# Local attention layers: keys transposed by VectorE in 32x32 blocks and DMAs instead of by TensorE, with another order of the query and key columns

## The chip, the cores and the metric

The kernel runs on one core of a Trainium2 chip. The metric is the device time of one execution in microseconds (us). The engines of the core work side by side, each through its own list of instructions in order: TensorE (PE; its weight loads are shown as PEld), VectorE (DVE), ScalarE (ACT), GpSimd (POOL) and SyncE (SP), which here issues nearly all DMAs. Sixteen DMA engines move what is issued.

## The reference, cut to what matters

The input x is 8 batches of 128 tokens of width 128. Four blocks of attention and feed-forward follow one another (L0 to L3). The change concerns the feed-forward parts of L2 and L3, which are themselves stacks of local attention layers: L2 has 6 layers with 16 heads of 64 and a window of 32, L3 has 2 layers with 8 heads and a window of 64. One layer of a stack:

```python
qkv = shift_tokens(x) @ Wqkv;  q, k, v = split(qkv)          # heads of 64
q = l2norm(q) * qs;  k = l2norm(k) * ksc
q = q * cos * scale + rotate_half(q) * sin * scale           # k: with 1 / scale
x = x + local_attention(q, k, v) @ Wo                        # softmax(8 q.k), a band of tokens
h = layernorm(shift_tokens(x)) @ W1 + b1
x = x + (a * gelu(gate)) @ W2 + b2                           # a, gate = halves of h
```

Scores sum over the 64 features of a head, so they do not depend on the order of the features, as long as queries and keys have the same order.

## The kernel before, in words

All of L2's and L3's work is one plan (`later_layers`, `plan_later`). Each step is added with `plan.add`: the engines that may do it with an assumed duration in ns (the account), the function that emits it, what it reads and writes, and for DMAs a `tail`, the time from the issue's end to landing. `Plan.arranged` then simulates the engines with this account and lets each engine take, of the steps that are ready, the one that was added first (its rank). The result is a fixed order of instructions on each engine. An instruction waits on semaphores for what it needs, and what stands behind it on its engine waits with it. SP's queue of DMA issues is such a list too.

A layer is worked batch by batch, in two parts. `Local.first` does `shifted` and `queries_keys`; `Local.rest` does `attention`. `some(n)` in `plan_later` adds the `rest` of a batch and before it the `first` of batches further on: two ahead in L2, one ahead in L3. After every two batches `gated` does the feed-forward part for the pair, and the next layer's batches become available. Weights of a layer are loaded by `weights`, alternating between two buffers. Where L2 ends, the steps of L3's cross attention (`l3x`) are woven in between the last batches of L2 and the first of L3 with `along`.

`queries_keys` handles tiles of 128 tokens x 512 columns (8 heads): in L2 two tiles of queries and two of keys per batch, in L3 one of each. Per tile: the projection on PE into PSUM (L1902), the squares on ScalarE (L1923), two products with the rotary tables on VectorE (L1924 with the cosines; L1926 with the sines, reading each head's halves swapped), the sum of squares per head on VectorE (L1928), and the sum of the two products on POOL (L1929). `inv_root` makes the inverse norms, and POOL multiplies each tile by them (L1942). Then the tile has to be transposed, features on the partitions:

- Queries go through `Blocks.turned`: VectorE transposes 32x32 blocks within the tile (L1795), SP issues four DMAs that put them, in runs of 128 floats (512 B), into a buffer in DRAM (L1799), and one DMA that reads the buffer back in rows of 2 KB (L1804). There are 8 such buffers, used in turn.
- Keys go through `Work.turn`: four TensorE transposes into a PSUM bank (L784), then a copy to SBUF by ScalarE (L771) or VectorE (L773), whichever the plan has free.

`weighed` computes the scores (band at L2010, products at L2016) and the exponentials (L2023); sums and outputs follow in `by_quarters` (L2077, L2083) or `by_halves` (L2056, L2062), the inverse (L2031 to L2040), the division (L2045), the output projection (L1991) and the update of y (L1995). In L2, `gated` moves the shifted rows by two DMAs (L2107), normalises, transposes through `Blocks.turned` as well (the tail of which is the ScalarE step at L2122), and runs the products L2132, L2146 and L2156.

Of the kernel before, what the change touches and what calls it, by code (L numbers as in the profile page):

```python
# [18 lines left out]
AF = mybir.ActivationFunctionType  # L19
ALU = mybir.AluOpType  # L20
AX = mybir.AxisListType
# [3 lines left out]
P = 128  # L25
# [59 lines left out]
def by_quarters(o):  # L85


    n = o.shape[1]
    o = o.reshape(2, 4, 2, 2, 32, n)
    return o.transpose(0, 2, 4, 3, 1, 5).reshape(P, 8 * n)  # L90


# [43 lines left out]
def laid_out(i):  # L136
# [60 lines left out]
    def local(m, qkv, wo, a, b):  # L197
# [15 lines left out]
        "experts": np.ascontiguousarray(experts), "expert_b2": i["L1_ffn_b2"],  # L213
        "l2a": l2a, "l2b": l2b, "l2o": l2o, "l3a": l3a, "l3b": l3b,
    }
# [508 lines left out]
class Work:  # L724
# [75 lines left out]
    def scaled(self, outs, ins, reads, writes, under, n=4, on_dve=False):  # L800
# [15 lines left out]

        plan.add({"POOL": (500 if on_dve else 930) + 150 * n}, root, [mv], [va] if on_dve else [va, nb])
        for k in range(n):
# [958 lines left out]
class Blocks:  # L1777
# [6 lines left out]

    def turned(self, t, n=4):

        w = self.w
        nc, plan = w.c.nc, w.plan
        room, val = self.rooms[self.turn][:, 0 : n * P], self.vals[self.turn]
        self.turn = (self.turn + 1) % len(self.rooms)  # L1790
        u, qT = w.tile([P, n * P]), w.tile([P, n * P])

        def within(e):
            flat = t().rearrange("p h d -> p (h d)")
            nc.vector.transpose(u().rearrange("p (c k j) -> p k c j", c=4, j=32), flat.rearrange("p (k c j) -> p k c j", c=4, j=32))  # L1795

        def out(e):
            for r in range(4):
                nc.sync.dma_start(room.rearrange("(c i) (r e) -> i c r e", c=4, r=4)[:, :, r, :],  # L1799
                                  u()[32 * r : 32 * r + 32].rearrange("p (c e) -> p c e", c=4))  # L1800

        plan.add({"DVE": 145 + 137 * n}, within, [t], [u])
        plan.add({"SP": 4 * 400}, out, [u], [val], tail=2100)
        plan.add({"SP": 400}, lambda e: nc.sync.dma_start(qT(), room), [val], [qT], tail=2300)  # L1804
        at = lambda k, lo, q, end, m=64: qT().rearrange("p (r k j) -> p k r j", r=4, j=32)[lo : lo + m, k, q // 32 : end // 32, :]
        return qT, at


BUFS_C = {"w": 2, "wr": 2, "tiny": 24, "few": 12, "row": 20, "big": 48}


class Local:
# [44 lines left out]
    def weights(self, l, after=(), begun=lambda load: None):  # L1857
# [14 lines left out]
        def emit(e):  # L1872
            for k, sname in enumerate(("_q_scale", "_k_scale")):
                s = c.get("row", self.name + sname, 64 * l, 64)
                nc.gpsimd.tensor_tensor(rot()[:, 2 * k, :], xpos[:, 2 * k, :], s, ALU.mult)
                for t in range(2):
                    lo, hi = 32 * t, 32 * (1 - t)
                    nc.gpsimd.tensor_tensor(rot()[:, 2 * k + 1, lo : lo + 32],
                                            xpos[:, 2 * k + 1, lo : lo + 32], s[:, hi : hi + 32], ALU.mult)

# [18 lines left out]
    def projected(self, layer, hs, j, o, opens):  # L1899
        nc = self.c.nc  # L1900
        ps, wqkv = self.bank([P, 512]), layer.wqkv
        self.plan.add({"PE": 860}, lambda e: nc.tensor.matmul(  # L1902
            ps(), lhsT=hs()[:, j, :], rhs=wqkv()[:, o : o + 512], start=True, stop=True), [hs, wqkv], [ps], "full", opens)
        return ps

    def queries_keys(self, layer, hs, j):
# [6 lines left out]
        for kind in range(2):  # L1913
            for g in range(ng):
                sq, t1, t2 = self.tile([P, 8, 64]), self.tile([P, 8, 64]), self.tile([P, 8, 64])
                ps = self.projected(layer, hs, j, kind * inner + g * 512, [t1])
                lo = 8 * (kind * ng + g)

                def emits(ps=ps, sq=sq, t1=t1, t2=t2, lo=lo, kind=kind):
                    heads = lambda: ps().rearrange("p (h d) -> p h d", d=64)  # L1920
                    halves = lambda v: v.rearrange("p h (t d) -> p h t d", t=2)
                    sin = lambda: spread(rot()[:, 2 * kind + 1, :].rearrange("p (t d) -> p t d", t=2), 8, 1)
                    yield lambda e: nc.scalar.activation(sq(), heads(), AF.Square)  # L1923
                    yield lambda e: nc.vector.tensor_tensor(t1(), heads(), spread(rot()[:, 2 * kind, :], 8, 1),  # L1924
                                                            ALU.mult)
                    yield lambda e: nc.vector.tensor_tensor(halves(t2()), halves(heads())[:, :, ::-1, :], sin(),  # L1926
                                                            ALU.mult)
                    yield lambda e: nc.vector.tensor_reduce(ss()[:, lo : lo + 8], sq(), AX.X, ALU.add)  # L1928
                    yield lambda e: nc.gpsimd.tensor_tensor(t1(), t1(), t2(), ALU.add)  # L1929

# [9 lines left out]
        for i in range(2 * ng):  # L1940
            t, t1 = self.tile([P, 8, 64]), ts[i]
            plan.add({"POOL": 1062}, lambda e, t=t, t1=t1, i=i: nc.gpsimd.tensor_tensor(  # L1942
                t(), t1(), spread(r()[:, 8 * i : 8 * i + 8], 64, 2), ALU.mult), [t1, r], [t])
            if i < ng:
                out.append(self.blocks.turned(t))
                continue
            tp = self.turn(lambda k, t=t: t().rearrange("p h d -> p (h d)")[:, k * P : (k + 1) * P], [t])
            kT = self.tile([P, 4, P])
            self.copy(kT, tp, [tp], [kT], 591, 682)
            out.append(kT)  # L1950
        return out[:ng], out[ng:]

    def inv_root(self, ss, n):

        nc, plan = self.c.nc, self.plan
        xh, r, t = (self.tile([P, n]) for _ in range(3))
        plan.add({"POOL": 240}, lambda e: nc.gpsimd.tensor_scalar(xh(), ss(), 1e-24, -0.5, ALU.max, ALU.mult), [ss], [xh])
        plan.add({"ACT": 215}, lambda e: nc.scalar.activation(t(), xh(), AF.Ln, scale=-2.0), [xh], [t], LOGS)
        plan.add({"ACT": 215}, lambda e: nc.scalar.activation(r(), t(), AF.Exp, scale=-0.5), [t], [r], LOGS)

# [18 lines left out]
    def attention(self, layer, b, hs, j, qTs, kTs):  # L1979
# [7 lines left out]
        for g, oT in enumerate(oTs):  # L1987
# [5 lines left out]

            plan.add({"PE": 890}, project, [oT, wr], [out], "full")
        plan.add({"DVE": 282}, lambda e: nc.vector.tensor_tensor(y(), y(), out(), ALU.add), [out, y], [y])  # L1995
# [31 lines left out]
    def inverse(self, sm):  # L2027

        nc, plan = self.c.nc, self.plan
        t, r = self.tile([P, 4, P]), self.tile([P, 4, P])  # L2030
        plan.add({"ACT": 597}, lambda e: nc.scalar.activation(t(), sm(), AF.Ln), [sm], [t], LOGS)  # L2031

# [4 lines left out]

        plan.add({"ACT": 632}, exp, [t], [r], LOGS)
        plan.add({"DVE": 688}, lambda e: nc.vector.tensor_tensor(sm(), sm(), r(), ALU.mult), [sm, r], [sm])
# [52 lines left out]
    def gated(self, l, b0, n, last=False):  # L2092
# [10 lines left out]
        if self.by_dma:  # L2103
# [4 lines left out]

            plan.add({"SP": 2 * 400}, move, ys, [moved], tail=2200)
            plan.add({"POOL": 150}, lambda e: nc.gpsimd.memset(sh()[0:1, :, 64:P], 0.0), [], [edge])  # L2110
# [8 lines left out]
        if self.by_dma:  # L2119
            hT, of_h = self.blocks.turned(sn, n)  # L2120
            hf = lambda: of_h(slice(0, n), 0, 0, P, P)
            plan.add({"ACT": 190 + 103 * n}, lambda e: nc.scalar.activation(hT(), hT(), AF.Identity, bias=offset, scale=gain), [hT], [hT])  # L2122
        else:
# [20 lines left out]
        for k, (lo, m) in enumerate(HCH):  # L2144
            pa, gl = self.bank([P, n * P]), gls[k]
            plan.add({"PE": 215 * n}, lambda e, pa=pa, lo=lo, m=m: nc.tensor.matmul(  # L2146
                pa()[:m], lhsT=w1()[:, lo : lo + m], rhs=hf(), start=True, stop=True), [hT, wr], [pa], "full")
            plan.add({"DVE": 145 + 150 * n}, lambda e, k=k, m=m, pa=pa, gl=gl: nc.vector.scalar_tensor_tensor(
                gl()[:m], pa()[:m], bias(k)[:m], gl()[:m], ALU.add, ALU.mult), [pa, gl], [gl])
# [62 lines left out]
def plan_later(w, route, l2x, l2, l3x, l3, stored):  # L2212
# [7 lines left out]
    def some(n):  # L2220

        for i in range(n):
            while at["first"] < min(at["rest"] + 1 + (2 if at["rest"] < 48 else 1), len(order)) and order[at["first"]] in given:
                loc, l, b = order[at["first"]]
                loc.first(l, b)
                at["first"] += 1
# [57 lines left out]
    pairs(l2, 5, 0, 4)  # L2284
    l2.end(0, 4)
    steps = l3x(0)
    along(steps, 0, 1)
    gated(l2, 5, 4, 2)
    along(steps, 1, 1)
# [4 lines left out]
    l2.end(4, 4)  # L2294
    l3.layers[1] = l3.weights(1)
    steps = l3x(1)
    for b in (0, 2):
        along(steps, 1, 1)
        gated(l3, 0, b, 2)
    for _ in steps:  # L2300
        pass
    begin(l3, 4, 4)
    pairs(l3, 0, 4, 4)
    for b, n in ((0, 1), (1, 1), (2, 1), (3, 1), (4, 2), (6, 1), (7, 1)):
# [25 lines left out]
def later_layers_any(c, a, wl, dram, route, wide, narrow, out):  # L2330
# [9 lines left out]
    with c.banks("psa_l2", mm=2, tp=2, sc=2, av=2):  # L2340
        local_layers_any(c, "L2_ffn", 6, 8, 32, a["l2a"], a["l2b"], room)
    with work(c, "l3x", BUFS_C, True) as w:
# [4 lines left out]
    with c.banks("psa_l3", mm=2, tp=2, sc=2, av=2):  # L2347
        local_layers_any(c, "L3_ffn", 2, 4, 64, a["l3a"], a["l3b"], room)
    store(c, out, 0, B)
# [43 lines left out]
```

## Time and profile before

| what | value |
|---|---|
| median of the runs | 1463.06 us (1461.44 to 1463.34, 3 runs) |
| the profiled execution, its own time | 1489.26 us |
| its span, first to last instruction | 1487.5 us |
| granted TensorE clock, mean | 0.964 |
| HBM traffic over the span | 95 GB/s |
| DMA packets | 148946, of which 34654 under 512 B |
| mean duration of a 128x512 VectorE product (L1924, L1926) | 675 ns |
| VectorE transpose of 128x512 (L1795) | 702 ns |
| POOL sum (L1929) and product (L1942) | 1276 and 1044 ns |

The profile is one execution. Its rows give, for a group of instructions: line, engine and operation, what is written <- what is read, shapes, count | busy us, mean ns of one | idle time of the engine just before them and what ended it. A row of a window gives its bounds and length, then each engine's busy time and count, the granted clock, the DMA engines' mean busy share and GB/s. A row of waits gives the total, the number and the longest, in us. A row of the chain of waits gives start, length and what the end of the program waited for at that moment.

### The profile page before, as it was taken

To read this page: it belongs to the slowest core of one execution; us is meant where nothing else is said; L and a number is where in the kernel's file an instruction comes from. 1 tells how busy PE (TensorE), PEld (TensorE's weight loads), DVE (VectorE), ACT (ScalarE), POOL (GpSimd) and SP (SyncE) were. 2 spreads that over 40 slices of the span, in tenths; PEclk is the share of its full clock that TensorE was granted. 3 is DMA by queue.
4 is the path that set the end of the run, shared out by engine and by line. 5 is a ranking of instruction groups with operands and counts; after the bars stand their busy time and mean duration, and the time that the engine had idled before them with its cause. 6 is when DMAs were issued, how large, how long until landed. Compare 5 with 4: busy or idle time off the path is not lost.

```text
span 1487.5 us, 40822 instructions
## 1 busy us (share of the span) xinstructions
PE 1391.6 (94%) x15943; PEld 984.0 (66%) x15943; DVE 1045.9 (70%) x2297; ACT 876.6 (59%) x1843; POOL 840.2 (56%) x1361
## 2 busy tenths in 40 slices
PE   9999998799889899999999999999999998899996
PEld 7777776666577566666666666666666667475765
DVE  7543774514358987888887978889888776678773
ACT  5665663054425657767665666656666566577573
POOL 5210334401346997777776767767787762638561
PEclk9999998899959999999999999999999999899997
DMA  9401001279440235235323323532433342212210
GB/s 310 157 1 43 2 3 49 78 256 359 142 147 5 58 97 166 67 76 160 95 73 111 96 75 78 163 89 68 124 94 90 89 132 81 65 28 63 56 48 24
DMA packets 148946, 145.77 MB, mean 98 GB/s; under 512 B 34654, under 2 KB 112030, under 8 KB 147592
## 3 DMA queue, kind: packets, MB, share of 16 engines
q1 hardware_dynamic: 142856, 137.83, 31.2%
q0 software_dynamic: 1536, 3.15, 0.7%
q8 instruction: 127, 2.08, 0.6%
q10 hardware_dynamic: 4352, 2.10, 0.5%
q14 instruction: 75, 0.61, 0.1%
HBM read 100.13 MB, written 41.32 MB: 95 GB/s over the span
## 4 chain that ended last, share of the span: by engine, by line
PE 43%; DVE 16%; POOL 9%; DMA 5%; ACT 4%; issue 4%; SPq 1%; another core or an unknown queue 1%; DVEq 0%; POOLq 0%; ACTq 0%
PE mm L1902 8%; PE mm L1991 5%; PE mm L784 5%; POOL big L1929 4%; DVE big L1924 3%; DVE big L1926 3%; DMA big<-blocks 3%; PE mm L2083 3%; PE mm L2132 2%; DVE few L1928 2%; PE mm L2016 2%; PE mm L2146 2%; PE mm L2156 2%; PE mm L791 2%; POOL big L1942 2%
## 5 line engine op out<-in xcount | busy, mean ns | idle before, releaser
L1929 POOL TENSOR_TENSOR big<-big,big 128x512 f32<-128x512 f32 x224 | 284.1, 1276 | 115.6 <-DVE big L1926 86.5
L771 ACT COPY big<-mm 128x512 f32<-128x512 f32 (+6 forms) x362 | 187.0, 527 | 217.7 <-PE mm L784 69.2
L1902 PE MATMUL mm<-wide,big 128*128 128x512 f32 x672 | 309.9, 599 | 1.2 <-DVE big L773 1.2
L1942 POOL TENSOR_TENSOR big<-big,few 128x512 f32<-128x512 f32 x224 | 227.4, 1044 | 2.1
L1902 PEld LDWEIGHTS mm<-wide,big 128*128 128x128 f32 x672 | 120.1, 191 | 117.5 <-issue 103.8
L1923 ACT ACTIVATE big<-mm 128x512 f32<-128x512 f32 x224 | 131.6, 595 | 86.8 <-PE mm L1902 76.3
L1924 DVE TENSOR_TENSOR big<-mm,big 128x512 f32<-128x512 f32 x224 | 151.1, 675 | 30.3 <-ACT big L1923 17.8
L784 PE MATMUL mm<-ident,big 128*128 128x128 f32 (+1 forms) x928 | 138.3, 283 | 18.7 <-DVE big L773 5.6
L784 PEld LDWEIGHTS mm<-ident,big 128*128 128x128 f32 (+1 forms) x928 | 106.1, 145 | 72.8 <-issue 20.6
L1926 DVE TENSOR_TENSOR big<-mm,big 128x512 f32<-128x512 f32 x224 | 151.2, 675 | 0.0
L1928 DVE TENSOR_REDUCE few<-big 128x8 f32<-128x512 f32 x224 | 149.6, 668 | 0.5 <-ACT big L1923 0.5
L773 DVE COPY big<-mm 128x512 f32<-128x512 f32 (+4 forms) x130 | 83.9, 662 | 78.7 <-PE mm L784 49.9
L2023 ACT ACTIVATE big<-mm 128x512 f32<-128x512 f32 x224 | 117.1, 609 | 17.7 <-PE mm L2016 17.7
L1991 PEld LDWEIGHTS mm<-narrow,big 128*128 128x128 f32 x896 | 107.7, 193 | 21.8 <-issue 6.5
L1991 PE MATMUL mm<-narrow,big 128*128 128x128 f32 x896 | 115.6, 280 | 5.5 <-DVE big L2045 3.6
L2016 PE MATMUL mm<-big,big 64*64 64x64 f32 (+2 forms) x3584 | 102.3, 240 | 6.4 <-DMA big<-blocks 6.4
L1795 DVE STREAM_TRANSPOSE big<-big 128x512 f32<-128x512 f32 (+1 forms) x136 | 87.4, 654 | 25.5 <-POOL big L1942 20.9
L2016 PEld LDWEIGHTS mm<-big,big 64*64 64x64 f32 x3584 | 96.2, 134 | 11.2 <-issue 5.6
L2083 PEld LDWEIGHTS mm<-big,big 128*32 128x32 f32 x3072 | 86.6, 110 | 24.5 <-issue 17.6
L2083 PE MATMUL mm<-big,big 128*32 128x128 f32 x3072 | 97.4, 273 | 0.0
L853 POOL TENSOR_TENSOR big<-big,tiny 128x308 f32<-128x308 f32 x41 | 28.9, 709 | 97.4 <-DVE tiny L850 75.8
L2045 DVE SCALAR_TENSOR_TENSOR big<-mm,big 128x512 f32<-128x512 f32 x112 | 73.7, 684 | 4.9 <-PE mm L2083 0.7
(300 smaller groups left out, 2568.3 us busy)
## 6 DMA issues: line engine op xcount, KB each, us to landing
big<-in_experts_dram SPq DMA_DIRECT2D x128, 256.0 KB
blocks<-big SPq DMA_DIRECT2D x448, 64.0 KB
big<-blocks SPq DMA_DIRECT2D x112, 256.0 KB
wide<-in_l2a_dram SPq DMA_DIRECT2D x6, 1536.0 KB
narrow<-in_l2b_dram SPq DMA_DIRECT2D x6, 534.0 KB
narrow<-in_l2o_dram SPq DMA_DIRECT2D x6, 512.0 KB
blocks<-big SPq DMA_DIRECT2D x96, 32.0 KB
big<-blocks SPq DMA_DIRECT2D x24, 128.0 KB
```

What stands on the lines that cost most here:

```text
L771: nc.scalar.copy(out(), in_())
L784: nc.tensor.transpose(tp()[:, k, :], v(k), c.ident)
L1902: self.plan.add({"PE": 860}, lambda e: nc.tensor.matmul(ps(), lhsT=hs()[:, j, :], rhs=wqkv()[:, o : o + 512], start=True, stop=True), [hs, ...
L1923: yield lambda e: nc.scalar.activation(sq(), heads(), AF.Square)
L1924: yield lambda e: nc.vector.tensor_tensor(t1(), heads(), spread(rot()[:, 2 * kind, :], 8, 1), ALU.mult)
L1926: yield lambda e: nc.vector.tensor_tensor(halves(t2()), halves(heads())[:, :, ::-1, :], sin(), ALU.mult)
L1928: yield lambda e: nc.vector.tensor_reduce(ss()[:, lo : lo + 8], sq(), AX.X, ALU.add)
L1929: yield lambda e: nc.gpsimd.tensor_tensor(t1(), t1(), t2(), ALU.add)
L1942: plan.add({"POOL": 1062}, lambda e, t=t, t1=t1, i=i: nc.gpsimd.tensor_tensor(t(), t1(), spread(r()[:, 8 * i : 8 * i + 8], 64, 2), ALU.mul ...
L1991: nc.tensor.matmul(out(), lhsT=oT()[:, k, :], rhs=wo()[:, 4 * g + k, :], start=(g == 0 and k == 0), stop=(4 * g + k == nch - 1))
L2016: nc.tensor.matmul(sc[s]()[at : at + 64, k, q:end], lhsT=kT()[lo : lo + 64, k, at : at + 64], rhs=of_q(k, lo, q, end), start=False, stop=( ...
L2083: nc.tensor.matmul(avs[half]()[32 * t : 32 * t + 32, k, :], lhsT=vs[t // 2]()[:, at : at + 32], rhs=prs[t]()[:, k, :], start=True, stop=True)
```

## The change

Keys take the path of the queries. `Blocks.turned` is split into a common part and three users: `queries`, `keys` and `rows` (the last for the gated half, as before). The columns of queries and keys inside each 512-wide tile are reordered in the weights, outside the kernel: from head, feature to four groups of 16 features, head, feature within the group (`by_sixteens`). In this order the VectorE transpose reads and writes its blocks in sequence. A query put writes runs of 128 floats as before. A key put writes runs of 32 floats (32 tokens), since the kernel reads keys with the four blocks of tokens side by side; that is 512 runs of 128 B in each of the four DMAs. The read back is as for queries.

With the new order the swap of a head's halves moves from VectorE's second product to POOL's sum, and the rotary tables are built to fit. In the account, durations of many steps are changed. `AHEAD` sets the look-ahead to two batches in L3 too. Where L2 ends and L3 begins, the order of the steps of the last two pairs and of `l3x` differs, and L3's second weight load is added later. The branch for unusual inputs, which does not run here, gets its own copy of the weights in the old order.

```diff
+def by_sixteens(w, inner):
+    out = w.copy()
+    groups = w[..., : 2 * inner].reshape(*w.shape[:-1], -1, 8, 4, 16)
+    out[..., : 2 * inner] = groups.swapaxes(-3, -2).reshape(*w.shape[:-1], 2 * inner)
+    return out
...
-    def turned(self, t, n=4):
+    def turned(self, n, within, room_of, u_of):
...
-        plan.add({"DVE": 145 + 137 * n}, within, [t], [u])
-        plan.add({"SP": 4 * 400}, out, [u], [val], tail=2100)
-        plan.add({"SP": 400}, lambda e: nc.sync.dma_start(qT(), room), [val], [qT], tail=2300)
+        plan.add({"DVE": 150 + 138 * n}, lambda e: nc.vector.transpose(*emit(u(), t())), [t], [u])
+        plan.add({"SP": 1880}, put, [u], [val], tail=1600)
+        plan.add({"SP": 400}, lambda e: nc.sync.dma_start(out(), room), [val], [out], tail=1800)
...
+    def keys(self, t):
+        kT = self.turned(4, (t, lambda u, t: (u, t.rearrange("p c g d -> p (c g d)"))),
+                         lambda room, r: room.rearrange("(i c) (k r j) -> i (c k) r j", c=4, k=4, r=4)[:, :, r, :],
+                         lambda u: u.rearrange("p (f j) -> p f j", j=32))
+        return self.w.plan.part(kT, lambda t: t.rearrange("p (k s) -> p k s", k=4))
...
-                    yield lambda e: nc.vector.tensor_tensor(halves(t2()), halves(heads())[:, :, ::-1, :], sin(),
-                                                            ALU.mult)
-                    yield lambda e: nc.vector.tensor_reduce(ss()[:, lo : lo + 8], sq(), AX.X, ALU.add)
-                    yield lambda e: nc.gpsimd.tensor_tensor(t1(), t1(), t2(), ALU.add)
+                    yield lambda e: nc.vector.tensor_tensor(t2(), heads(), by(1), ALU.mult)
+                    yield lambda e: nc.vector.tensor_reduce(ss()[:, lo : lo + 8], sq().rearrange("p c g d -> p g c d"), AX.XY, ALU.add)
+                    yield lambda e: nc.gpsimd.tensor_tensor(halves(t1), halves(t1), halves(t2)[:, ::-1, :], ALU.add)
...
-            if i < ng:
-                out.append(self.blocks.turned(t))
-                continue
-            tp = self.turn(lambda k, t=t: t().rearrange("p h d -> p (h d)")[:, k * P : (k + 1) * P], [t])
-            kT = self.tile([P, 4, P])
-            self.copy(kT, tp, [tp], [kT], 591, 682)
-            out.append(kT)
+                t(), t1(), spread(spread(r()[:, 8 * i : 8 * i + 8], 16, 2), 4, 1), ALU.mult), [t1, r], [t])
+            out.append(self.blocks.keys(t) if i >= ng else self.blocks.queries(t))
...
-            plan.add({"SP": 2 * 400}, move, ys, [moved], tail=2200)
+            plan.add({"SP": 1570}, move, ys, [moved], tail=2300)
...
-            while at["first"] < min(at["rest"] + 1 + (2 if at["rest"] < 48 else 1), len(order)) and order[at["first"]] in given:
+            while at["first"] < min(at["rest"] + 1 + AHEAD, len(order)) and order[at["first"]] in given:
...
+    pairs(l2, 5, 4, 2)
     steps = l3x(0)
-    along(steps, 0, 1)
-    gated(l2, 5, 4, 2)
     along(steps, 1, 1)
     gated(l2, 5, 6, 2)
...
-    for b in (0, 2):
-        along(steps, 1, 1)
+    for b, counts in ((0, (2, 2)), (2, (1, 0))):
+        along(steps, *counts)
         gated(l3, 0, b, 2)
```

## The prediction

> **What bounds the kernel now.** I read the page first: TensorE (PE) is busy for 94% of the span, VectorE (DVE) 70%, ScalarE (ACT) 59%, GpSimd (POOL) 56%.
>
> ```profile
> PE 1391.6 (94%) x15943; PEld 984.0 (66%) x15943; DVE 1045.9 (70%) x2297; ACT 876.6 (59%) x1843; POOL 840.2 (56%) x1361
> ```
>
> That is a mean over stages, so next I cut out one layer of L2. The update of y at L1995 comes once per layer and batch; every eighth starts at 873.7, 999.5 and 1125.3 us, so a layer lasts 125.8 us. All six L2 layers together run from about 492 to 1235 us. The second row is what follows them, L3x's rest and L3.
>
> ```profile
> core 0: us, PE busy (x) PEld busy (x) DVE busy (x) ACT busy (x) POOL busy (x), PEclk, DMA share, GB/s
> 873.70:999.50 125.80, 122.32 (x1545) 83.17 (x1545) 106.33 (x198) 81.83 (x158) 92.00 (x138) 1.00 0.36 98
> 1190.00:1487.50 297.50, 266.14 (x2771) 188.42 (x2770) 200.14 (x453) 185.74 (x407) 156.81 (x285) 0.93 0.22 62
> ```
>
> In a layer PE idles 3.5 us and VectorE 19.5 us: PE bounds it. After L2 PE idles 31 us of 297.5. Third, the groups of that layer:
>
> ```profile
> L1929 POOL TENSOR_TENSOR big<-big,big 128x512 f32<-128x512 f32 x32 | 40.5, 1277 | 18.2 <-DVE big L1926 17.2 <-PE mm L2083 1.0
> L1942 POOL TENSOR_TENSOR big<-big,few 128x512 f32<-128x512 f32 x32 | 32.4, 1046 | 0.3
> L771 ACT COPY big<-mm 128x512 f32<-128x512 f32 (+2 forms) x30 | 15.6, 526 | 14.6 <-PE mm L1902 11.1 <-PE mm L784 3.4
> L1795 DVE STREAM_TRANSPOSE big<-big 128x512 f32<-128x512 f32 (+1 forms) x20 | 12.5, 646 | 2.1 <-POOL big L1942 1.9
> L784 PE MATMUL mm<-ident,big 128*128 128x128 f32 x65 | 9.5, 277 | 0.4 <-DVE big L2045 0.2
> L773 DVE COPY big<-mm 128x512 f32<-128x512 f32 x10 | 6.7, 688 | 8.9 <-PE mm L784 8.9
> ```
>
> A layer has 16 key tiles (8 batches, two groups of heads). L784 is their 64 TensorE transposes. Of the 16 copies out of PSUM VectorE does 10 (L773), ScalarE 6 (its 30, less 16 of values and 8 of the shifted input). L1795 is the 16 query transposes and 4 smaller ones of the gated half. Fourth, the chain of waits, in a dense place of PE and where L3 begins:
>
> ```profile
> 650.54 0.44 PE mm L784 x4
> 650.98 0.86 PE mm L1902 x2
> 651.84 0.44 PE mm L784 x4
> ...
> 1283.64 0.63 DVE big L1795
> 1285.91 1.79 DMA blocks<-big
> 1287.85 2.55 DMA big<-blocks
> 1290.53 1.97 PE mm L2016 x24
> ```
>
> A key tile holds PE for 0.44 us, not 4 x 277 ns, because the four overlap. The lower rows show a transposed query exposed: 6.9 us from its VectorE transpose to the scores.
>
> **What the change removes.** PE: 16 x 0.44 = 7.0 us per layer, so 122.3 becomes 115.3. The 16 copies go: ScalarE loses 6 x 0.58 = 3.5 us, VectorE 10 x 0.60 = 6.0 us (a 128x512 operation lasts about 0.68 us, but one starts every 0.60 us in a dense row of them). A PSUM bank per key tile is no longer taken; I credit nothing for it.
>
> **What it adds.** VectorE: 16 transposes of 702 ns (the mean of the 128x512 form of L1795), 0.62 each after the overlap: 9.9 us. Net 106.3 + 3.9 = 110.2 us.
>
> SyncE (SP): five more DMAs per key tile, four puts and a read. A query's puts start 0.48 us apart and the read's issue takes about 0.40, so 2.3 us per tile, 37 per layer. SP now issues 111 DMAs of 0.46 us mean in the layer, 51 us; that becomes 88. They stand in SP's one queue ahead of the gated half's puts and reads (L1799, L1804), its shifted rows (L2107) and the weight loads.
>
> The engines of the DMA: a key put moves runs of 32 tokens, 128 B, so a tile has 2048 packets where a query has 512, and then 128 packets of 2 KB back. No packets of 128 B are in this trace. Three short stretches hold almost one size each: 256 B (shifted rows), 512 B (query puts), 2048 B (reads).
>
> ```profile
> 654.00:654.40 0.40, 0.40 (x2) 0.16 (x2) 0.40 (x2) 0.37 (x1) 0.40 (x1) 1.00 0.60 131
> 649.80:650.00 0.20, 0.20 (x2) 0.00 (x0) 0.20 (x2) 0.20 (x1) 0.20 (x1) 1.00 0.76 177
> 656.50:657.10 0.60, 0.60 (x3) 0.29 (x2) 0.60 (x3) 0.49 (x1) 0.43 (x1) 1.00 1.03 396
> ```
>
> Share x 16 engines x size / rate gives 19, 35 and 85 ns per packet. The line through the first two puts 128 B at 11 ns; its upper bound by a row is a 256 B packet's 19. I take 14, nearer the line. Then a tile costs 2048 x 14 / 16 + 128 x 85 / 16 = 1.8 + 0.7 = 2.5 us of all engines, 40 us per layer on the present 0.36 x 125.8 = 45: a share of 0.71 in a layer of 120.
>
> Here a rule speaks against the change. The Trainium skill (DMA: Bandwidth & Descriptors, Specifications) says that a transfer needs 512 B or more for line rate and that below it the engine reads, modifies and writes. Were a 128 B packet therefore as dear as a 512 B one, 35 ns, a put would last 32 x 35 = 1.12 us instead of 0.48. The row with 256 B at 19 ns already contradicts a floor at 512 B, so the sum goes by the row; the rule is the slow rival below.
>
> **What it moves or leaves.** Where the queries' and keys' columns lie in another order, the same elements are handled: L1924, L1926, L1928 and the POOL pair keep their counts. VectorE's runs shrink from 64 and 32 to 16; L1924 (runs of 64) and L1926 (32, halves swapped) both take 675 ns, so I take no cost; one engine step per run would bound it at about 30 ns each, 3 us per layer. For L1942, L1225 (four runs of 128) takes 1041 ns against 1046 with eight of 64, so I take nothing; its bound is L1929's 1277, 7 us per layer, and POOL would still be at 83%. A gain is not excluded for the transpose, whose two sides are now in order; I take 0. The wait that moves: scores now wait for a key's DMA too. Two batches of look-ahead, some 30 us, cover 7 us inside L2; in L3 the look-ahead becomes two as well. Without cover it is bare where a stack begins. There the keys' multiply ends 1.05 us after the queries', and their puts queue behind: about 2.3 us more each time. Account durations, the order of L2's end with L3x, and the place of L3's second weight load change the order of the planned instructions: I take 0, bounds 10 us each way, since PE idles 31 us after L2. The extra weight copies belong to the branch that does not run.
>
> **Sum.** A layer: PE's 115.3 plus idle. With VectorE at 92% of the layer instead of 85%, I let the idle grow from 3.5 to 5: 120.3, so -5.5 x 6 = -33 us. L3's 16 tiles: -16 x 0.44 x 0.89 (PE's share there) = -6.3, and one and a half bare waits of 2.3 give +3.3: -3. Together -36 on the profiled execution's own 1489.3 (span 1487.5): 1453. The median, 1463.06, is 0.982 of the profiled time, so -35 there: **1428 us**.
>
> **Rivals.** (1) VectorE takes half of it. For: in the chain, runs of VectorE operations stand 0.60 us apart for 14 us (from 620 us on), and there a fourth kind of work joins. Against: it still has 15 us idle per layer. Were PE to idle 9 us, a layer lasts 124.3: -1.5 x 6 = -9, with L3's -3 it is -12: **1451**.
>
> (2) The gated half waits longer. Of the waits within 492 to 1235 us, first ScalarE's, then one of SP's own queue:
>
> ```profile
> ACT big L2122 <- DMA big<-blocks: 35.6, 13, 4.9
> ```
>
> ```profile
> SPq L1804 <- DMA blocks<-big: 42.6, 71, 2.5
> ```
>
> The first is ScalarE standing before the gated half's tile with its exponentials queued behind. PE waits 15.3 us at L2132 for that, a share of 0.43. A batch's two key tiles are put one after the other, so each of L2's 24 gated groups may meet one to two of them, 2.5 us each. At 1.5 that is 90 us on ScalarE and 39 on PE, and with all three borders bare (3.7 more): 1428 + 42 = **1470**. At 1.2 it is **no change**. Against it: SP would still be free for a quarter of a layer, and the planner lets the step with the lowest rank go first.
>
> (3) The transfer queue becomes the bound. SP must hold 51 us plus 16 tiles in the 120 us that PE would leave: 4.3 us per tile, 3.9 for four puts, 0.97 per put, and 32 packets per engine make that 30 ns per packet. From there on it decides. At the rule's 35 ns: 16 x (4 x 1.12 + 0.4) + 51 = 129 us; with the DMA engines then near full (45 + 16 x (4.5 + 0.7) = 128) and reads waiting behind puts, some 133 per layer: +7 x 6, **1505**.
>
> **Chances.** Forecast 0.53 (1405 to 1443), rival 1 0.15 (1443 to 1460), no change 0.05, rival 2 above it 0.13 (1466 to 1480), rival 3 0.14 (1480 to 1545). A measurement can tell about 0.2%, 3 us, from no change. Range 1405 to 1478: the low end adds 10 us of order and a PE that idles no more than now. The likeliest case alone is 1405 to 1443.
>
> **What would show it.** Right: a layer of about 120 us between y updates, L784 at some 480 matmuls instead of 928, L1795's line with 112 more of about 0.7 us, VectorE near 92% in a layer, the DMA share near 0.7, packets under 512 B up by 229,000 (112 tiles x 2048). Rival 1: PE idle over 7 us per layer, waiting for VectorE. Rival 2: L2122's wait doubled. Rival 3: SP's DMA instructions well over 0.46 us each, scores (L2016) waiting for the DMA. I am wrong if 128 B packets cost 30 ns or more, or if scores wait inside L2.

## The result and the profile after

The changed kernel takes 1633.24 us (median of 4 runs, 1631.96 to 1638.21) against 1462.25 us for the kernel before on the same chip (1455.62 to 1463.34): a ratio of 1.119, 95% interval 1.115 to 1.123. The forecast was 1428 us, or 0.976. The profiled execution took 1633.65 us (span 1631.7 us), 144 us more than the span before. In some sessions the kernel before takes 1462 to 1467 us and in others 1487 to 1490, at a lower granted clock (about 0.97 against 0.98), so ratios are always to its runs in the same session, and the profile of before, with 1489 us, is of the slower kind.

The page of the changed kernel first: busy times, the shares of the chain that ended last, and the DMA packets.

```profile
PE 1384.5 (85%) x15507; PEld 961.6 (59%) x15507; DVE 1082.1 (66%) x2355; ACT 851.9 (52%) x1784; POOL 843.3 (52%) x1366
...
PE 47%; DVE 16%; DMA 11%; POOL 9%; SPq 7%; issue 5%; ACT 4%; DVEq 0%; POOLq 0%; ACTq 0%
...
DMA packets 401624, 204.55 MB, mean 125 GB/s; under 512 B 272990, under 2 KB 350366, under 8 KB 400264
```

Every engine has a smaller share than before, so none of the five took TensorE's place. In the chain, which had 5% DMA and 1% SPq (SyncE's queue) before, they now have 11% and 7%. Two layers of L2, each cut from an update of y (now L2019) to the eighth after it (columns as in the rows of before):

```profile
802.10:952.40 150.30, 122.58 (x1482) 82.79 (x1480) 110.23 (x206) 79.33 (x154) 91.08 (x137) 0.92 0.55 135
952.40:1101.40 149.00, 124.69 (x1481) 83.29 (x1480) 110.02 (x207) 79.33 (x151) 93.02 (x141) 0.92 0.60 142
```

A layer lasts 150 us instead of 125.8. TensorE has some 63 matmuls less, and now idles 24 to 28 us per layer; its granted clock is 0.92 instead of 1.00, so that it is busy as long as before. VectorE is at 110 us, as forecast, and the DMA engines are a little over half busy.

From the first to the last of L2's 48 updates of y it is 867 us where it was 737, 130 more; what follows takes 31 us more, and what stands ahead 17 less. Part of the 31 is work that the new order moves out of L2: with the account and order alone (`e7_before_plan`, below) the two stretches take 720 and 252 us against 867 and 266 here. So the rest of the change costs 147 us in L2, some 24 per layer, and 14 after it.

What TensorE and the others wait for is in the waits of the whole run (total us, times, longest us). Before, a row of the page (the scores, with their waits behind the last bar) and one of the waits:

```profile
L2016 PE MATMUL mm<-big,big 64*64 64x64 f32 (+2 forms) x3584 | 102.3, 240 | 6.4 <-DMA big<-blocks 6.4
```

```profile
ACT big L2122 <- DMA big<-blocks: 36.1, 14, 4.9
```

And after:

```profile
ACT big L2146 <- DMA big<-blocks: 88.0, 21, 11.0
DVE few L813 <- DMA big<-y_res: 86.7, 19, 9.1
...
PE mm L2040 <- DMA big<-blocks: 73.8, 29, 8.4
...
PEld mm L2040 <- DMA big<-blocks: 38.9, 14, 8.7
```

L2146 is ScalarE's step of the gated half (L2122 before, 36.1 us), L813 the statistics of its shifted rows, L2040 the scores (L2016 before, 6.4 us). All three wait for transfers that SP issues. So the next view is SP's own timeline (start us, us, line, count), first eight puts of the kernel before, then a stretch of the first of these layers:

```profile
648.93 3.74 SPq L1799 DMA_DIRECT2D blocks<-big  x8
```

```profile
838.26 0.46 SPq L1808 DMA_DIRECT2D big<-blocks  x1
838.76 3.17 SPq L1803 DMA_DIRECT2D blocks<-big  x4
842.10 0.46 SPq L1808 DMA_DIRECT2D big<-blocks  x1
842.61 2.58 SPq L1803 DMA_DIRECT2D blocks<-big  x4
845.30 0.54 SPq L1808 DMA_DIRECT2D big<-blocks  x1
```

SP issues put after put with hardly a gap. Four puts hold it for 2.6 to 3.2 us, where the kernel before issued eight in 3.74. The duration of a put's issue (ns, min/median/max, over all puts of the run), before and after:

```profile
L1799 SPq DMA_DIRECT2D blocks<-big x544: 302/434/1909, 488.8 to 1451.8; - x182
```

```profile
L1803 SPq DMA_DIRECT2D blocks<-big x992: 320/600/1907, 469.7 to 1594.5; - x199
```

The median put went from 434 to 600 ns, and the queries' puts with it (mean 0.453 to 0.634 us), though they still move 128 runs of 512 B. In a layer SP issues about 190 DMAs that last 111 to 116 us together, with some 12 us of small gaps (under 0.2 us) between them; in the remaining 21 to 27 us it waits. Before it was 111 DMAs and 51 us.

The forecast's cheap items did come out. By groups of one form:

```profile
L1806 DVE STREAM_TRANSPOSE big<-big 128x512 f32<-128x512 f32 x224 | 152.6, 694 | 15.5 <-POOL big L1972 13.5 <-PE mm L2101 0.3
L1972 POOL TENSOR_TENSOR big<-big,few 128x512 f32<-128x512 f32 x224 | 231.1, 1059 | 2.3 <-DMA blocks<-big 0.5
L1956 DVE TENSOR_TENSOR big<-mm,big 128x512 f32<-128x512 f32 x224 | 151.9, 678 | 75.2 <-ACT big L1955 38.3 <-PE mm L1934 36.4
```

### The profile page after: what moved, and what is told of

Read it like the earlier page. It is cut to its first block, busy times and chain, and to the rows that moved or that the text cites. A ratio compares the mean times of both kernels' runs of the same rounds, so it can differ in the third digit from the quotient of the medians.

```text
span 1631.7 us, 41015 instructions
## 1 busy us (share of the span) xinstructions
PE 1384.5 (85%) x15507; PEld 961.6 (59%) x15507; DVE 1082.1 (66%) x2355; ACT 851.9 (52%) x1784; POOL 843.3 (52%) x1366
## 4 chain that ended last, share of the span: by engine, by line
PE 47%; DVE 16%; DMA 11%; POOL 9%; SPq 7%; issue 5%; ACT 4%; DVEq 0%; POOLq 0%; ACTq 0%
PE mm L1934 7%; DMA big<-blocks 6%; SPq L1803 6%; PE mm L799 4%; PE mm L2040 3%; PE mm L792 3%; PE mm L2156 3%; PE mm L2015 3%; PE mm L2107 3%; DVE big L1956 3%; PE mm L2170 2%; POOL big L1972 2%; DVE big L1957 2%; DVE few L1958 2%; PE mm L2101 2%
## 5 line engine op out<-in xcount | busy, mean ns | idle before, releaser
L779 ACT COPY big<-mm 128x512 f32<-128x512 f32 (+6 forms) x294 | 149.3, 517 | 168.9 <-PE mm L792 49.1
L1972 POOL TENSOR_TENSOR big<-big,few 128x512 f32<-128x512 f32 x224 | 231.1, 1059 | 2.3 <-DMA blocks<-big 0.5
L2040 PE MATMUL mm<-big,big 64*64 64x64 f32 (+2 forms) x3584 | 118.9, 264 | 86.3 <-DMA big<-blocks 73.8
L1806 DVE STREAM_TRANSPOSE big<-big 128x512 f32<-128x512 f32 (+1 forms) x248 | 161.7, 668 | 18.7 <-POOL big L1972 13.5
L2040 PEld LDWEIGHTS mm<-big,big 64*64 64x64 f32 x3584 | 105.7, 152 | 102.6 <-issue 47.6
L2015 PE MATMUL mm<-narrow,big 128*128 128x128 f32 x896 | 116.3, 282 | 10.9 <-DVE big L2069 8.5
L2107 PEld LDWEIGHTS mm<-big,big 128*32 128x32 f32 x3072 | 95.0, 114 | 33.1 <-issue 26.9
L2156 PE MATMUL mm<-big,narrow 128*128 128x256 f32 x174 | 59.8, 491 | 60.6 <-ACT big L2146 54.5
L792 PE MATMUL mm<-ident,big 128*128 128x128 f32 (+1 forms) x480 | 72.9, 289 | 19.6 <-DVE big L781 5.2
L2156 PEld LDWEIGHTS mm<-big,narrow 128*128 128x128 f32 x174 | 35.9, 223 | 80.5 <-ACT big L2146 59.0
L792 PEld LDWEIGHTS mm<-ident,big 128*128 128x128 f32 (+1 forms) x480 | 56.2, 149 | 44.0 <-DVE big L781 10.5
L2034 PE MATMUL mm<-band_L_ffn,identb 64*64 64x512 bf16 x448 | 60.6, 418 | 24.3 <-DVE big L1957 24.3
```

The lines of the kernel that those rows point to most:

```text
L779: nc.scalar.copy(out(), in_())
L792: nc.tensor.transpose(tp()[:, k, :], v(k), c.ident)
L1806: plan.add({"DVE": 150 + 138 * n}, lambda e: nc.vector.transpose(*emit(u(), t())), [t], [u])
L2015: nc.tensor.matmul(out(), lhsT=oT()[:, k, :], rhs=wo()[:, 4 * g + k, :], start=(g == 0 and k == 0), stop=(4 * g + k == nch - 1))
L2040: nc.tensor.matmul(sc[s]()[at : at + 64, k, q:end], lhsT=kT()[lo : lo + 64, k, at : at + 64], rhs=of_q(k, lo, q, end), start=False, stop=( ...
L2107: nc.tensor.matmul(avs[half]()[32 * t : 32 * t + 32, k, :], lhsT=vs[t // 2]()[:, at : at + 32], rhs=prs[t]()[:, k, :], start=True, stop=True)
```

## The experiments

What differs between a put before and a put after? The source is the same: 32 partitions, in 4 pieces of 512 B (or, for keys, 16 of 128 B). The destination in DRAM is not. Before, rows are numbered `(c i)`, and its pieces form a block of 4 x 32; in the new order they are numbered `(i c)`, so that all pieces lie one pitch apart and form one single run of 128 (keys: 512). I call the first form a block and the second merged. In the expectations, theory A says that SP's issue time is the cause, B the small packets on the DMA engines, C the wrong durations in the account; later D, that VectorE's added transposes are the floor, E, that the column order or the new order of steps is what costs, and F, that the gated half's transfers wait in SP's queue behind the puts. Ratios are to the kernel before; one run each where no interval is given.

**The account alone** (`e1_put_account`):

```diff
-        plan.add({"SP": 1880}, put, [u], [val], tail=1600)
-        plan.add({"SP": 400}, ..., [val], [out], tail=1800)
+        plan.add({"SP": 2700}, put, [u], [val], tail=1600)
+        plan.add({"SP": 500}, ..., [val], [out], tail=2300)
```

> The changed kernel with one difference: the planner's account gives the four puts 2700 ns instead of 1880 and the read 500 + 2300 instead of 400 + 1800, which is what they took in the trace. Theory A (SyncE's queue is full: 190 DMAs of some 0.6 us per L2 layer and the gaps between them): the same issues have to be made, so the time stays within 3%, 1590 to 1650. Theory C (the order was built on durations that are too short, so instructions wait in the wrong place): most of the loss goes, 1500 or less.

Measured 1614.3 us, ratio 1.100. A planner that knows the cost of a put gains one to two per cent and leaves the rest: C is not the main cause.

**Queries' puts as a block again** (`e2_queries_unmerged`) and **both kinds as a block** (`e3_all_unmerged`; the keys' source in 512 B runs as well, decay factors set to one):

```diff
-   lambda room, r: room.rearrange("(i c) (r e) -> i c r e", c=4, r=4)[:, :, r, :],
+   lambda room, r: room.rearrange("(c i) (r e) -> i c r e", c=4, r=4)[:, :, r, :],
```

> The changed kernel, but the queries' puts go to the rows of the kernel before (block c to rows 32c + i instead of 4i + c), so that their destination is again 4 x 32 runs and not one run of 128. The queries' features then stand in another order than the keys', so the scores are not the reference's; the work is the same. Theory A: such a put issues in 0.44 us instead of 0.60, 64 puts per L2 layer save 10 us or more, 60 us in L2 and 10 in L3: about 1560. Theory B (the 128 B packets load the DMA engines): the packets of the keys are all there, so 1620 to 1640.

> The changed kernel with both the queries' and the keys' puts as 4 x 32 runs of 512 B (block c to rows 32c + i). Queries and keys then hold wrong features for their places, and the decay tables are set to 1 so that the wrong scores stay small; the number of instructions and DMAs is unchanged. Theory A: every put issues in 0.44 to 0.48 us as before the change, which is the case that the forecast worked out: 1430 to 1480. Theory B: also 1430 to 1480, so this run is read together with the keys' puts of 512 B alone. Theory C: 1430 to 1500, since the account's 1880 ns is then right.

Measured 1569.7 us (1.070) and 1504.7 us (1.025). In the first, the queries' puts fell to a median of 0.435 us and the keys' stayed at 0.627. The second is above the range of each theory, though all puts are at the old cost:

```profile
L1803 SPq DMA_DIRECT2D blocks<-big x992: 302/436/2572, 474.1 to 1466.7; - x199
```

**Keys in runs of 512 B, but merged** (`e4_keys_512`), the counterpart: the keys' put takes the form of the queries', with a quarter of the packets.

```diff
-   lambda room, r: room.rearrange("(i c) (k r j) -> i (c k) r j", c=4, k=4, r=4)[:, :, r, :],
-   lambda u: u.rearrange("p (f j) -> p f j", j=32))
+   lambda room, r: room.rearrange("(i c) (r e) -> i c r e", c=4, r=4)[:, :, r, :],
+   lambda u: u.rearrange("p (c e) -> p c e", c=4))
```

> The changed kernel with the keys' puts made like the queries' puts of the changed kernel: runs of 512 B, 128 packets per DMA instead of 512, with the same merged destination. The keys' tokens then stand in the wrong places, and the decay tables are set to 1. Theory A: the issue stays at 0.60 us, so the time stays within 2% of the changed kernel, 1600 to 1640. Theory B: three quarters of the keys' packets are gone and with them most of the loss, 1550 or less.

Measured 1619.4 us, 1.104. Without a single packet of 128 B the kernel is nearly as slow, and the issue is as long:

```profile
L1803 SPq DMA_DIRECT2D blocks<-big x992: 321/598/1990, 470.3 to 1580.5; - x199
```

B falls; A holds. The issue's length goes with the destination's form and hardly with the number of packets: 0.60 us with 128 of them, 0.63 with 512. `e3_all_unmerged` differs from this run in the form of the destinations alone.

But even at 0.44 us per put the kernel is 2.5% slower than before, not 2.4% faster. So there is a second cause. Is it VectorE and TensorE, or still the queue?

**Keys turned by VectorE, with no DMA at all** (`e5_keys_no_dma`; queries as a block; the keys' blocks stay where the transpose leaves them), **keys by TensorE as before, queries in the new form** (`e6_keys_on_pe`), and **the kernel before with only the account, the look-ahead and the new order** (`e7_before_plan`):

```diff
-        kT = self.turned(4, ...)
+        kT = w.tile([P, 4 * P])
+        w.plan.add({"DVE": 150 + 138 * 4}, lambda e: w.c.nc.vector.transpose(kT(), t()...), [t], [kT])
```

```diff
+            tp = self.turn(lambda k, t=t: t().rearrange("p c g d -> p (c g d)")[:, k * P : (k + 1) * P], [t])
+            kT = self.tile([P, 4, P])
+            self.copy(kT, tp, [tp], [kT], 591, 682)
```

> The changed kernel without the keys' DMAs: VectorE's blockwise transpose of each key tile stays and its result is used as it is, so the keys are only transposed within blocks and the scores are not the reference's (decay tables set to 1); the queries' puts go to 4 x 32 runs, which issue in 0.44 us. PE is relieved of the key transposes and VectorE has the added ones, as in the changed kernel, and SyncE's queue is as light as in the kernel before. Theory A (SyncE's queue alone ate the gain): the forecast's sum without its transfer terms, 1415 to 1440. Theory D (VectorE's added transposes are the floor): 1463 or more.

> The changed kernel with the keys back on TensorE, copied out of PSUM by ScalarE or VectorE as in the kernel before; the column order, the queries' merged puts (0.60 us per issue), the account and the order of the stages are the changed ones. The key tiles' columns are taken in sequence, so a key holds features of other heads and the scores are not the reference's (decay tables set to 1). Theory A: SyncE has 111 DMAs per L2 layer again, some 62 us, and PE is the bound as before: 1455 to 1485. Theory E (the column order or the new order of stages is what costs): well above, 1520 or more.

> The kernel before with only the changed account, the look-ahead of two in L3 and the changed order of steps at L2's end and L3's start; keys on TensorE, old column order. Theories A and B: within 1% of the kernel before, 1450 to 1475. Theory E: a large part of the loss is here, 1500 or more.

Measured: 0.9765 (0.9708 to 0.9822), 1.0067 (1.0047 to 1.0086), 0.9931 (0.9906 to 0.9955). The first is the figure that I forecast for the whole change (0.976): the exchange of TensorE for VectorE is worth its price once its DMAs are away, so D falls. The second is the third with the new column order, and so with merged puts for the queries: 1.0067 against 0.9931, a price of about 1.4% with not one key in the queue. The third says that the account and the order gain 0.7% by themselves, where I took 0; so E falls too. And the exchange itself is worth 0.9765 / 0.9931, some 1.7% and not 2.4%: that the first lands on my figure is in part luck.

**Fewer, larger puts** (`e8_paired`): in L2, two tiles share one put and the column order takes groups of 8 features. Per pair there are four puts (256 runs of 512 B, or 1024 of 128 B) and two reads; durations in the account as measured; the pool `big` holds 39 tiles instead of 48 to make room. The reference's output is computed.

```diff
+                    nc.sync.dma_start(room.rearrange("(i c) (r e) -> i c r e", c=8, r=4)[:, :, r, :],
+                                      part.rearrange("p (c e) -> p c e", c=8))
```

> The changed kernel with L2's two query tiles of a batch put by four DMAs together, and its two key tiles too (columns in eight groups of 8 features, so that 1024 columns make one buffer of 256 rows; runs of 128 floats and of 32 tokens as before, the same number of packets), with two reads each, and the account set to the measured durations. SyncE then issues 12 DMAs per batch for queries and keys instead of 20, some 84 us per L2 layer with the gaps instead of 125. Theory A (issues): most of the loss goes, 0.97 to 1.02 of the kernel before. Theory B (packets, or their landing): as many packets of 128 B as in the changed kernel, so 1.08 or more.

Measured 1.0258 (1.0216 to 1.0301), just above A's range and far below B's. A put of twice the packets takes 0.611 us (queries, median) or 0.704 (keys), so half the puts go for little more each. Yet the kernel stays as slow as with cheap puts. What both leave in the queue shows in SP's timeline of `e3_all_unmerged`:

```profile
1028.55 1.91 SPq L1803 DMA_DIRECT2D blocks<-big  x4
1030.62 0.34 SPq L1808 DMA_DIRECT2D big<-blocks  x1
1031.01 1.90 SPq L1803 DMA_DIRECT2D blocks<-big  x4
1033.02 1.45 SPq L1808 DMA_DIRECT2D big<-blocks  x1
1034.51 1.61 SPq L2131 DMA_DIRECT2D big<-y_res  x2
1036.36 0.35 SPq L1808 DMA_DIRECT2D big<-blocks  x1
```

The shifted rows of the gated half (L2131) stand behind these two groups of four puts and two reads, the second of which takes 1.45 us to issue, and behind others before them. The second of the two updates of y that they copy was done at 1021.48 us:

```profile
1021.23 0.25 DVE L2019 TENSOR_TENSOR y_res<-y_res,mm 128x128 f32<-128x128 f32 x1
```

So they were issued 13.0 us after they could have been. Over L2's 24 pairs the median of this delay is 0.1 us in the kernel before, 16.1 in the changed one (with 23 DMAs issued in between), 10.9 here, and 7.7 in `e8_paired`. The waits in the same kernel:

```profile
ACT big L2146 <- DMA big<-blocks: 64.4, 22, 7.8
...
PE mm L2040 <- DMA big<-blocks: 24.0, 16, 6.3
```

The scores' wait has fallen from 73.8 to 24.0 us, ScalarE's at the gated half only from 88.0 to 64.4. That leads to theory F.

**The gated half off SP's queue**, shifted and turned by TensorE as L3's already is, in four kernels: `e3` with it (`e9_unmerged_gated_pe`), the plan alone with it (`e10_before_plan_gated_pe`), the changed kernel itself (`e11_after_gated_pe`), and the paired puts (`e12_paired_gated_pe`, the reference's output):

```diff
-        self.by_dma = nch == 8
+        self.by_dma = False
```

> The run with all puts as 4 x 32 runs of 512 B (wrong features, decay tables set to 1), which lay at 1.025 of the kernel before, with the gated half of L2 taken off SyncE's queue: its shift and its transpose are done by TensorE, as in L3. That takes some 28 DMAs of 190 from SyncE and adds some 2 us to PE per L2 layer. Theory F (what was left of the loss is the gated half's transfers queued behind the keys'): 0.96 to 0.99. Theory A alone (only the sum of issues counts, 99 us falling to 84): 1.00 to 1.01.

> The kernel before with the changed account and order (0.993 of it) and the gated half of L2 on TensorE as well; keys on TensorE. The gated half no longer waits for DMAs (35 us of ScalarE's time), PE has 2 us more per layer. Theory F's other side: if the wait costs the kernel before as well, 0.98 to 0.99; if PE's time counts, 1.00.

> The changed kernel with one line changed: the gated half of L2 shifts and transposes on TensorE, so that SyncE has about 28 DMAs fewer per L2 layer. The keys' and queries' puts stay as the change made them. Theory A: SyncE's queue goes from about 125 us per layer to about 105, still over what all-unmerged puts had (99), so 1.02 to 1.06 of the kernel before. Theory F (the wait of the gated half was nearly all of it): below 1.00.

> Paired puts in L2 and the gated half of L2 on TensorE together, everything else as in the changed kernel; the output is the reference's. SyncE has about 98 DMAs per L2 layer, no more than the kernel before, and nothing of the gated half stands in its queue, while PE is free of the key transposes. Theories A and F: 0.97 to 0.985 of the kernel before, faster than both kernels. Theory B (packets of 128 B): 1.01 or more.

Measured 0.9812 (0.9771 to 0.9853), 0.9940 (0.9919 to 0.9960), 1.0557 (1.0522 to 1.0591) and 0.9787 (0.9755 to 0.9818). The same edit that brings nothing to the kernel before (0.9931 to 0.9940) brings 4.4 to 6.3 points where the keys' DMAs share the queue (1.025 to 0.981, 1.119 to 1.056). So F holds where puts are cheap or few. In `e11_after_gated_pe`, with the dear puts, it does not: F asked for less than 1.00, and 1.056 lies in A's range. There the scores still wait:

```profile
PE mm L2040 <- DMA big<-blocks: 98.1, 39, 7.4
```

The edit also takes some 28 of 190 DMAs out of the queue, so it does not separate what stood in the queue from how full the queue was. What speaks for the place in it is the delay above, and that `e8_paired`, whose DMAs last some 80 us in a layer, is no faster than `e3_all_unmerged` with 90. B falls once more with `e12_paired_gated_pe`, which moves all the packets of 128 B.

Laid out with the put's form, as ratios to the kernel before:

| a put's issue | gated half through SP | gated half by TensorE |
|---|---|---|
| 0.60 us (merged, as changed) | 1.119 | 1.056 |
| 0.44 us (block) | 1.025 | 0.981 |
| half as many, 0.61 to 0.70 us | 1.026 | 0.979 |

Removing one cause alone does not turn the sign; without both, the kernel is 1.9 to 2.1% faster than before, of which the account and the order alone give some 0.6% (`e10_before_plan_gated_pe`). A layer in `e9_unmerged_gated_pe`, then in `e12_paired_gated_pe`:

```profile
858.60:977.70 119.10, 116.45 (x1498) 77.45 (x1497) 109.18 (x207) 77.28 (x151) 91.85 (x135) 1.00 0.60 166
```

```profile
874.30:993.50 119.20, 116.47 (x1497) 77.96 (x1496) 109.25 (x207) 77.22 (x151) 92.42 (x135) 1.00 0.68 164
```

Both last 119.1 to 119.2 us, TensorE idles 2.7 us of it at full clock, and SP's DMAs last 72 us in the first (163 of them) and 65 in the second (99) instead of 111 to 116. `e12_paired_gated_pe`, which computes all of the reference, takes less time than both kernels of this case.

## Why the prediction was wrong

**The step that failed is SyncE's term.** I wrote: "A query's puts start 0.48 us apart and the read's issue takes about 0.40, so 2.3 us per tile, 37 per layer", and had SP go from 51 to 88 us. The 0.48 was read from puts with a block as destination, and I carried it over to a form that no row showed. I also let the queries' puts stay as they were, since they "write runs of 128 floats as before", although the diff turns their `(c i)` into `(i c)`. With what was measured: 16 key tiles x (4 x 0.63 + 0.47) = 48 us, and the 16 query tiles 16 x (4 x 0.18 + 0.13) = 14 us more than they were; 51 + 48 + 14 = 113 us, which is the 111 to 116 seen. With the small gaps of 12 us that is about 125 us, more than the layer of 120 that TensorE would have left; with the 21 to 27 us in which the queue waits it is the 150 measured. The second step that failed is the same queue's delay for what else stands in it (rival 2, below).

**Rival 3 had the place right, the mechanism half and the price wrong.** It made the queue the bound through packets of 30 ns or more, and gave 1505. Packets of 128 B took 13.4 ns in the mean (229,376 of them; I took 14), and those of 512 B 32 ns. The rule that I weighed there, read as a floor at 512 B, would have made them as dear as those; my line through the rows was right, and no such floor shows. The bound came from the issue instead. Its own test, "0.97 per put", was not met by 0.63 only because the test left the queries' puts at the old cost: with 65 us instead of 51 for the rest, a tile has (120 - 65) / 16 = 3.4 us, less 0.47 for the read, so 0.74 per put. The gaps of 12 us leave 0.55, and the 0.63 of a key's put is over that edge. The signs that I had named for it did appear: SP's DMAs went from 0.46 to 0.60 us in the mean, and scores wait inside L2.

**"Two batches of look-ahead, some 30 us, cover 7 us inside L2" failed with it.** A look-ahead covers a latency, not a queue that is full. A put landed 2.11 us (queries) or 2.48 us (keys) after its issue began, in the median, where a query's took 1.78 before; yet the scores waited 73.8 us in all.

**Rival 2 was true beside it, and under-priced.** I dismissed it as "SP would still be free for a quarter of a layer". In `e3_all_unmerged` SP's DMAs last 90 us of a layer of 125 to 130, so it is free for about that share, and ScalarE still waits 64.4 us at the gated half: in a queue kept in order, what stands ahead at that moment counts. I gave it 0.5% (1470); taking the gated half off the queue is worth 4.4 points there (1.025 to 0.981). Its sign came too: the wait at the gated half, 36.1 us before, is 88.0.

**What held.** TensorE at 115.3 us per layer: 116.5 in `e9` and `e12`, whose gated half adds TensorE work. VectorE at 110.2: 109.2 to 110.2 in the layers shown, so the transpose at 694 ns, the products at 678 and POOL's at 1059 bore out the terms I took at no cost. A layer of 120.3: 119.1, where the queue is free; but from `e10` to `e9` only L2's middle layers gain this (125.6 to 119.1), the last stretch of L2 does not (114.0 to 115.8), so that 27 us came out between these two profiled executions and not 36. Packets under 512 B: up by 238,336, which are the 229,376 and 16 small ones of 4 B for each of the 560 added DMAs. DMA share 0.71 of 120 us: 0.55 to 0.60 of 150, which is 83 to 89 us against 85. Rival 1 did not appear: TensorE idles 2.7 us per layer with VectorE at 92%.

**A term that I did not have:** in the starved layers TensorE's clock was 0.92, and its 1482 matmuls were busy for 123 us where 1498 took 116.5 at 1.00. So up to 7 us per layer of the 24 may go with the clock. That it fell because TensorE idled is argued, not shown: I know it only from rows side by side (0.89 to 0.93 in the changed kernel's layers, 0.97 to 0.99 in `e3`, 1.00 in `e9` and `e12`).

**Two slips that decide nothing.** L2's last update of y starts at 1252.6 us, later than the 1235 at which I let L2 end, and one and a half waits of 2.3 us are 3.5, not 3.3.

**What stays open.** Not shown are the reason why a merged destination is dearer to issue, what makes the 14 us after L2, where I took -3, and how much of F is the delay and how much the lighter queue. A key put with the right rows and a block as destination was not tried, since it takes a pattern of one dimension more than these transfers have; nor was another engine's queue for the keys' puts.

## What to carry to other kernels

Before work moves from an engine to DMAs, sum the time of the queue that issues them as for any engine, by the issue durations in its own timeline, and only from transfers of the same form on both sides; a reordering of columns that costs the engines nothing can change the form of transfers that nobody meant to touch. A queue in order that is about three quarters full can already delay what is urgent in it by ten microseconds, as here, so ask who stands behind the new work, and move the urgent transfers away or make fewer, larger ones. Check how near the bound the one resource comes that the page of busy shares does not list: here it was SP.

## What the hardware showed that I had not expected

- The issue of a put from SP takes 0.44 us with a 4 x 32 destination (the kernel before, `e3_all_unmerged`) and 0.60 to 0.63 with the same bytes as one run of pieces, whether 128 or 512; with twice the bytes, 256 pieces take 0.61 and 1024 take 0.70 (`e8_paired`). The Trainium skill (Perfetto Trace Analysis, What "DMA-bound" means) says of a full DMA sequencer that its slices are descriptor generation and that large descriptors are what matters. Here pieces four times as large (`e4_keys_512`) changed a key's put from 627 to 598 ns and the ratio from 1.119 to 1.104, while the form of the destination and fewer DMAs brought it to about 1.025; so for this queue the measurement decides against it.
- Packets of 128 B took 13.4 ns in the mean of the changed kernel's run, of 256 B 18, of 512 B 32, of 2 KB 105: no step at 512 B.
- The reads' issue grew as well, from 0.34 to 0.47 us (medians), with no change to their form; it is 0.34 again in `e3_all_unmerged`, where the puts are blocks. The Trainium skill (Perfetto Trace Analysis, DMA Instruction — HWDGE) has an instruction's profiled time include its wait for the descriptor generator; whether the reads wait for that, no run here shows.
